# Two cross attentions on one core: products of the identity in the last steps, and the last image outputs added by VectorE

## The chip, the cores and the metric

The kernel runs on one core of a Trainium2 chip. The metric is the time of one execution on the device in microseconds (us). The engines of the core work side by side, each through its own queue of instructions in order: TensorE (products and transpositions), VectorE, ScalarE, GpSimd, and SyncE, which issues most of the transfers.

## What is computed

Two cross attentions in a row, each with 20 heads of 16 channels, over 64 batch entries of 256 tokens and 320 channels, all in float32. The context of an entry has 77 rows of 512 channels. The first attention, cut to what matters:

```python
q, k, v = x @ Wq.T, text @ Wk.T, text @ Wv.T      # by head
out = softmax(q @ k.T / 4) @ v                    # 77 rows of context
x = merge_heads(out) @ Wo.T + bo + x
```

The second treats the last 4 rows of the context as an image:

```python
probs_t = softmax(q @ k_t.T / 4)                  # 73 text rows
text_out = probs_t @ v_t
qsem = l2norm(probs_t @ text)
fused = q @ k_ip.T / 4 + 0.5 * (qsem @ l2norm(ip).T)
ip_out = (softmax(fused) * mask) @ v_ip           # 4 image rows
out = (merge(text_out) + merge(ip_out)) @ W_out + b_out + x
```

The change touches where `merge(ip_out)` is added to `merge(text_out)`, and nothing else that is computed.

## The kernel before, in words

Two batch entries make a pair; there are 32 pairs (NP). A pair takes 10 steps (NU) in each layer: two entries times five units, a unit being eight (entry, head, token block) blocks. The loop at the end of the function runs over steps g from 0 to 344. In step g the first layer works on unit g and the second on unit g - 13 (LAG). So the first layer ends with step 319 and the second layer's scores with step 332; steps 333 to 344 only finish the last pair. The order of instructions on each engine is the order in which the program issues them (keep_order), so a waiting instruction holds back everything behind it on its engine.

One step of the second layer is this. `semantics` (L744, L750) multiplies the transposed weights of the step before with a table of the context and the values; `scores` (L641) multiplies queries and keys. Both write one tile of four PSUM banks, `sc`, of which there is a single buffer. VectorE reads it three times: the maximum (`mx`, L659), the subtraction (`w`, L661), and the product with the weights (`prod`, L761 and L764). ScalarE copies its text sums (`sums`, L1096). Only then may the next step's products write the tile. ScalarE takes the exponential (L672, L673), and TensorE transposes the result in the next step: `transposed` (L705 into `tr`, L706 into `rtr`), copied out by ScalarE (L712, L713). The tiles of all transpositions come from one pool of two buffers, handed out in turn. A transposition is a single instruction `nc.tensor.transpose(to, data, ident)`.

Other work of the pairs is put into the steps by `fillers`, in four lists. Those that matter in the last steps are, with k = g % 10: `queries` (L555 to L570), `text_transposed` (k = 0 and 5; `atr`, L826, copied by L829 and L830), `gram` (k = 6, L493), `image_transposed` (k = 7; `itr`, L903, copied to `iwT` by L905), `image_attend` and `image_attend_last` (k = 8; `ipv`, L915 and L932), `project` (k = 9; `o_ps`, L528, its end L537 in the next step, results added to x by L601), and `project_last` (k = 0 and 2; L616, added by L620). At the end of an entry (step k = 4 or 9 of the second layer's count) its image weights are made: `image_least`, `image_norm` (a square root and an exponential on ScalarE, each with a table load, L863 and L865), `image_scores`, `image_shifted`, `image_exponential` and `image_weights` (L871 to L891 and L839), over ScalarE, VectorE and GpSimd in turn; `text_output` makes `an`, which `text_transposed` reads.

`image_attend` writes two banks (`both`). Its `out_of` has ScalarE copy each to `t` in SBUF (L921), and after the second GpSimd adds all of `t` to the main part of `aT` (L923), which `project` reads.

Of the kernel before, what the change touches and what calls it, by code (L numbers as in the profile page):

```python
# [8 lines left out]
F32 = mybir.dt.float32  # L9
# [13 lines left out]
P = 128  # L23
# [15 lines left out]
NU = 2 * len(UNITS)  # L39
# [24 lines left out]
def tile_two_cross_attentions(ctx: ExitStack, tc: tile.TileContext, a: dict, out: bass.AP):  # L64
# [35 lines left out]
    nc = tc.nc  # L100
    x_in, c_in, cip_in = a["x"], a["ctx"], a["ctx_ip"]
    NB = x_in.shape[1] // S
    NP = NB // 2
# [8 lines left out]
    ptr = ctx.enter_context(tc.tile_pool(name="ptr", bufs=2, space=PSUM))  # L112
# [95 lines left out]
    def load_more(g):  # L208
        queue = nc.sync
        if g == 1:  # L210
            queue.dma_start(cip, cip_in.rearrange("(k p) t -> p k t", p=P))
            load_ctx_weight("wkip1", queue, wkip)
        elif g == 3:
            load_ctx_weight("wvip1", queue, wvip)
        elif g == 5:
            wo[0], bo[0] = load_out("wo0", queue), load_bias("bo0", queue)
        elif g == 6:
            wq[1] = load_chan("wq1", queue)
        elif g == 8:
            wo[1], bo[1] = load_out("wo1", queue), load_bias("bo1", queue)  # L220
            queue.dma_start(smask, a["smask"])


    ident = const.tile([P, P], F32, tag="ident", name="ident")
# [99 lines left out]
    kTs, kbds, qs, vips, aTs = {}, {}, {}, {}, {}  # L324
# [304 lines left out]
    def eight(t, u):  # L629

        return t[:, PLACES[u] : PLACES[u] + 8].rearrange("p (r e) ... -> p r e ...", e=2)
# [65 lines left out]
    def transposed(l, p, b, u, w):  # L697

        n = P if l else 8 * R0
        part, s = UNITS[u]  # L700
        flat = w.rearrange("p i j t -> p (i j t)") if l else w
        ps = ptr.tile([P, 4, P], F32, tag="tr", name=f"tr{l}_{p}_{b}{u}")
        pr = ptr.tile([P, 4, P], F32, tag="tr", name=f"rtr{l}_{p}_{b}{u}")
        for i in range(4):
            nc.tensor.transpose(ps[:, i, :], flat[:, i * P : (i + 1) * P], ident)  # L705
        nc.tensor.transpose(pr[:n, 0, :], flat[:, 4 * P : 4 * P + n], ident)  # L706
        if l:
            pts[1] = (
                sp.tile([P, 4, P], F32, tag="pt1", name=f"pt1_{p}_{b}_{u}"),
                sp.tile([n, P], F32, tag="pr1", name=f"pr1_{p}_{b}_{u}"),  # L710
            )
            nc.scalar.copy(pts[1][0], ps)  # L712
            nc.scalar.copy(pts[1][1], pr[:n, 0, :])  # L713
            return
        if part == 2:
            pt, rt = pts[0, 2, b] = (
                sp.tile([P, 2, S], F32, tag="pt2", name=f"pt2_{p}_{b}"),
                sp.tile([n, P], F32, tag="pr2", name=f"pr2_{p}_{b}"),
            )
            nc.scalar.copy(  # L720
                pt.rearrange("p l (s t) -> p s l t", s=2), ps.rearrange("p (s l) t -> p s l t", s=2)
            )
            nc.scalar.copy(rt, pr[:n, 0, :])
            return
        if s == 0:
            pts[0, part] = (
                sp.tile([P, 4, S], F32, tag="pt0", name=f"pt0_{p}_{b}_{part}"),
                sp.tile([n, S], F32, tag="pr0", name=f"pr0_{p}_{b}_{part}"),
            )
        pt, rt = pts[0, part]  # L730
        nc.scalar.copy(pt[:, :, s * P : (s + 1) * P], ps)  # L731
        nc.scalar.copy(rt[:, s * P : (s + 1) * P], pr[:n, 0, :])

    def semantics(ps, start, stop, p, b, u, rows):

        part, _ = UNITS[u]
        pt, rt = rows
        for i in range(4):  # L740
            for j in range(2):
                half_rows = slice(j * M, (j + 1) * M)
                at = SEM0 + i // 2 * GV
                nc.tensor.matmul(  # L744
                    ps[:, i % 2 * 2 + j, at : at + GV], pt[half_rows, i, :], gv[b][half_rows, part, i, :],
                    start=start and i < 2, stop=False,
                )
        for r in range(4):
            quarter = slice(r * QR, (r + 1) * QR)
            nc.tensor.matmul(  # L750
                ps[:, r, SEM0 : SEM0 + 2 * GV].rearrange("p (e d) -> p e d", d=GV)[:, :, M:],
                rt[quarter, :], gr[b][quarter, part], start=False, stop=stop,
            )
# [154 lines left out]
    def image_attend(p):  # L908

        wT = made["wT"]  # L910
        both = [pms.tile([P, 512], F32, tag="ms", name=f"ipv{p}_{i}") for i in range(2)]
        for b in range(2):
            for i in range(2):
                rows = slice(i * QR, (i + 1) * QR)
                nc.tensor.matmul(  # L915
                    both[i][:, b * S : (b + 1) * S], vips[p, b][rows, i * P : (i + 1) * P],
                    wT[rows, b * S : (b + 1) * S], start=True, stop=True,
                )

        def out_of(i):  # L920
            nc.scalar.copy(t[:, i, :], both[i])  # L921
            if i:
                nc.gpsimd.tensor_add(aTs[1, p][0], t, aTs[1, p][0])  # L923

        t = big.tile([P, 2, S2], F32, tag="ip_out", name=f"ip_out{p}", bufs=1)
        return [lambda i=i: out_of(i) for i in range(2)]
# [110 lines left out]
    def unit(g):  # L1037
        return (g // NU, g % NU // len(UNITS), g % len(UNITS)) if 0 <= g < NP * NU else None
# [11 lines left out]
    for g in range(NP * NU + LAG + 12):  # L1050
        p, k = divmod(g, NU)
        first, second, third, begin = fillers(k, p)
        if g == NU + 3:
            in_order = len(nc.cur_bb.bb.instructions)
        load_more(g)
        now = [unit(g), unit(g - LAG)]
        ps = prod = None
        for fn, args in early.pop(g, ()):
            fn(*args)
        drains = [fn for what in ("q", "o") if what in held for fn in held.pop(what)()]  # L1060
        if now[0] or now[1] or before1:
            ps = psc.tile([P, 4, 512], F32, tag="sc", name=f"sc{g}")
            todo = []
            if before1:
                todo.append((semantics, (*before1[:3], before1[4])))
            for l in range(2):
                if now[l]:
                    todo.append((scores, (l, *now[l])))
            for n, (fn, args) in enumerate(todo):
                fn(ps, n == 0, n == len(todo) - 1, *args)  # L1070
        for fn, args in begin:
            fn(*args)
        if "i" in held:
            drains += held.pop("i")()
        for fn in drains:
            fn()
        for l in range(2):
            if now[l]:
                shifted(ps, l, *now[l])
        new1 = None  # L1080
        if last1:
            transposed(1, *last1)
            new1 = (*last1, pts[1])
        if now[0] and k != 5:
            exponential(0, g, *now[0])
        if before1:
            prod = weighted(ps, *before1[:4])
        for fn, args in first:
            fn(*args)
        if last0:  # L1090
            transposed(0, *last0)
        if now[0] and k == 5:
            exponential(0, g, *now[0])
        ends = before1 and before1[2] == len(UNITS) - 1
        if before1:
            nc.scalar.copy(eight(stats[before1[:2]][1], before1[2]), by_block(ps)[:, :, :, TT:])  # L1096
            if ends:
                image_least(*before1[:2])
        if now[1]:
            exponential(1, g, *now[1])  # L1100
        for fn, args in later.pop(g, ()):
            fn(*args)
        if now[0]:
            normalize(g)
        if before1:
            q, b, u = before1[:3]
            nc.vector.tensor_reduce(eight(stats[q, b][2], u), prod, AX.X, ALU.add)  # L1107
            if ends:
                image_squares(q, b)
                made["an"] = text_output(q, b)  # L1110
                later[g + 1] = [(image_scores, (q, b))]
                early[g + 2] = [(image_shifted, (q, b)), (image_exponential, (q, b))]
                early[g + 3] = [(image_weights, (q, b))]
        for fn, args in second:
            fn(*args)
        if last0:
            q, b, u, _ = last0
            if u == 1 or u == len(UNITS) - 1:
                attend(q, b, int(u > 1))
        for fn, args in third:  # L1120
            fn(*args)
        if ends:
            image_norm(*before1[:2])
        last0 = (*now[0], ws[0]) if now[0] else None
        before1 = new1
        last1 = (*now[1], ws[1]) if now[1] else None
# [51 lines left out]
```

## Time and profile before

| | us |
|---|---|
| median of 3 runs (2629.02 to 2631.37) | 2630.31 |
| the profiled execution's own time | 2628.61 |
| its span, first to last instruction | 2626.9 |
| TensorE busy | 2549.2 (97%) |
| VectorE busy | 1969.9 (75%) |
| ScalarE busy | 1538.8 (59%) |
| GpSimd busy | 1442.4 (55%) |
| TensorE's share of the chain that ended last | 87% |
| mean granted clock of TensorE | 0.986 |

A matmul's end is modelled, so neighbouring matmuls overlap in the records; how fast they follow each other is read from their starts. A product in float32 leaves two records, a transposition one. The page cuts the span into 40 equal slices of 66 us; a digit is the busy share in tenths, and the row PEclk is the share of TensorE's full clock that was granted. In a timeline a row has its start, its length, engine, line and tiles, and in brackets the idle time before it and what ended it. In a table of stretches each row is one stretch, with busy time and count for each engine, then the granted clock, the share of the transfer engines and GB/s.

### The profile page before, as it was taken

The numbers are of one execution on the slowest core, as the hardware profiler recorded it, in microseconds if no ns is written. First come the engines' busy times: TensorE is split into PE (matmuls) and PEld (weight loads), VectorE is DVE, ScalarE is ACT, GpSimd is POOL, SyncE is SP. The second block draws the span as 40 slices with busy tenths as digits, with TensorE's granted clock in tenths as the row PEclk, the third lists the DMA queues.
The fourth block names the chain that finished last, engine by engine and source line by source line (L and its number), as shares of the span: only waits on it lengthen the run. The fifth ranks groups of instructions, "written<-read, shape, count | busy, mean of one in ns | idle before, by whom it ended". The sixth has DMA issues, their size and how long they took to land.

```text
span 2626.9 us, 73603 instructions
## 1 busy us (share of the span) xinstructions
PE 2549.2 (97%) x26792; PEld 1974.0 (75%) x26792; DVE 1969.9 (75%) x3639; ACT 1538.8 (59%) x3991; POOL 1442.4 (55%) x3515
## 2 busy tenths in 40 slices
PE   7999999999999999999999999999999999999897
PEld 5677777777777777777777777777777777777675
DVE  3577777777777777777777777777777777777864
ACT  3465665655665665665665665655665655665643
POOL 2455555565555565555565555565555565555542
PEclk9999999999999999999999999999999999999986
DMA  5212211112111112111112111112111112111000
GB/s 163 72 29 58 58 42 47 42 51 57 57 44 47 42 51 58 58 42 48 42 52 57 58 42 48 41 52 58 58 42 48 41 52 58 56 38 36 26 22 23
DMA packets 154657, 132.24 MB, mean 50 GB/s; under 512 B 48249, under 2 KB 132985, under 8 KB 154297
## 3 DMA queue, kind: packets, MB, share of 16 engines
q1 hardware_dynamic: 153432, 126.38, 16.8%
q8 instruction: 215, 3.52, 0.5%
q10 hardware_dynamic: 864, 1.15, 0.1%
q14 instruction: 146, 1.19, 0.1%
HBM read 89.53 MB, written 33.91 MB: 47 GB/s over the span
## 4 chain that ended last, share of the span: by engine, by line
PE 87%; DVE 6%; ACT 3%; DMA 1%; issue 1%; POOL 1%; SPq 0%; POOLq 0%; DVEq 0%; ACTq 0%
PE sc L744 13%; PE tr L705 11%; PE o_ps L528 8%; PE sc L641 7%; PE v_ps L379 6%; PE sc L750 5%; PE q_ps L555 4%; PE q_ps L528 4%; PE k_ps L334 4%; PE o_ps L616 3%; PE o_ps L537 3%; PE pv L777 2%; DVE w L661 2%; PE q_ps L557 2%; PE q_ps L563 2%; PE rtr L706 2%
## 5 line engine op out<-in xcount | busy, mean ns | idle before, releaser
L659 DVE TENSOR_REDUCE mx<-sc 128x8 f32<-128x584 f32 (+1 forms) x640 | 497.6, 778 | 460.1 <-PE sc L641 460.0
L692 POOL TENSOR_TENSOR parts<-w,sm 128x512 f32<-128x512 f32 (+1 forms) x640 | 439.6, 708 | 301.6 <-ACT parts L673 180.7
L661 DVE TENSOR_TENSOR w<-sc,mx 128x616 f32<-128x616 f32 x640 | 511.9, 800 | 66.7 <-DVE mx L659 0.5
L712 ACT COPY pt<-tr 128x512 f32<-128x512 f32 x320 | 186.8, 584 | 449.3 <-PE tr L705 437.5
L705 PE MATMUL tr<-ident,parts 128*128 128x128 f32 x2560 | 412.8, 284 | 12.8 <-POOL parts L692 5.2
L744 PEld LDWEIGHTS sc<-gv,pt 64*128 64x128 f32 x5120 | 323.5, 191 | 117.2 <-ACT sums L1096 67.5
L744 PE MATMUL sc<-gv,pt 64*128 64x94 f32 x5120 | 363.3, 282 | 35.1 <-ACT sums L1096 32.7
L705 PEld LDWEIGHTS tr<-ident,parts 128*128 128x128 f32 x2560 | 284.5, 142 | 124.6 <-issue 88.8
L676 POOL COPY att<-w 128x32 f32<-128x32 f32 x320 | 66.8, 209 | 469.7 <-DVE w L661 469.0
L669 ACT ACTIVATE w<-w 128x616 f32<-128x616 f32 x320 | 232.0, 725 | 96.3 <-DVE w L661 95.4
L687 DVE TENSOR_REDUCE sm<-w 128x8 f32<-128x616 f32 x320 | 248.2, 776 | 13.5 <-ACT w L669 13.5
L641 PE MATMUL sc<-kbd,q 32*128 32x154 f32 x5120 | 250.0, 308 | 1.0 <-ACT q L586 0.8
L528 PE MATMUL o_ps<-aT,wo 128*128 128x256 f32 x1024 | 234.3, 383 | 1.6 <-POOL aT L923 1.6
L1107 DVE TENSOR_REDUCE nrm<-prod 128x8 f32<-128x584 f32 x320 | 227.4, 711 | 0.4
L761 DVE TENSOR_TENSOR prod<-sc,parts 128x512 f32<-128x512 f32 x320 | 218.0, 681 | 5.5 <-PE sc L750 5.5
L528 PEld LDWEIGHTS o_ps<-aT,wo 128*128 128x128 f32 x1024 | 192.0, 193 | 25.8 <-POOL aT L923 2.4
L672 ACT ACTIVATE parts<-w 128x512 f32<-128x512 f32 x320 | 206.8, 646 | 0.0
L641 PEld LDWEIGHTS sc<-kbd,q 32*128 32x128 f32 x5120 | 188.5, 188 | 6.0 <-issue 5.0
L731 ACT COPY pt<-tr 128x512 f32<-128x512 f32 x256 | 150.6, 588 | 67.5 <-PE tr L705 66.8
L379 PE MATMUL v_ps<-wv,cf 128*128 128x320 f32 (+1 forms) x624 | 182.1, 438 | 0.0
L706 PE MATMUL rtr<-ident,parts 128*104 128x128 f32 (+1 forms) x640 | 175.9, 275 | 0.0
L1096 ACT COPY sums<-sc 128x168 f32<-128x168 f32 x320 | 96.6, 302 | 118.9 <-DVE prod L764 118.0
(148 smaller groups left out, 4802.9 us busy)
## 6 DMA issues: line engine op xcount, KB each, us to landing
vip<-vip_rows SPq DMA_DIRECT2D x1280, 5.0 KB
out_dram<-x SPq DMA_DIRECT2D x64, 256.0 KB
x<-in_x_dram SPq DMA_DIRECT2D x31, 512.0 KB
v_rows<-vs SPq DMA_DIRECT2D x38, 320.0 KB
vm<-v_rows SPq DMA_DIRECT2D x152, 80.0 KB
ct<-in_ctx_dram SPq DMA_DIRECT2D x32, 308.0 KB
cf<-in_ctx_dram SPq DMA_DIRECT2D x38, 256.0 KB
g_rest<-gram_rest SPq DMA_DIRECT2D x512, 0.5 KB
```

The costliest lines, as they stand in the source:

```text
L379: nc.tensor.matmul(ps[:n, :C], cfs[i][:, k, :n], wv[l][:, k, :], start=(k == 0), stop=(k == KE - 1))
L528: nc.tensor.matmul(ps[b][:, m, :], w[:, k, m * P : (m + 1) * P], main[:, k, b * S : (b + 1) * S], start=(k == 0 and m == 0), stop=False,)
L641: nc.tensor.matmul(ps[:, r, 2 * T * l : 2 * T * (l + 1)], q[rows, b, :] if part == 2 else q[rows, t0 : t0 + P], kbd[rows, part].rearrange( ...
L659: nc.vector.tensor_reduce(mx, sc[:, :, :, :nt], AX.X, ALU.max)
L661: nc.vector.tensor_tensor(w, sc, mx.unsqueeze(3).broadcast_to([P, 4, 2, T]), ALU.subtract)
L669: nc.scalar.activation(w, w, AF.Exp, scale=SCALE)
L687: nc.vector.tensor_reduce(sm, w, AX.X, ALU.add)
L692: nc.gpsimd.tensor_tensor(two[:, 8 * t0 : 8 * t1].rearrange("p (h t) -> p h t", h=8), w[:, :, t0:t1], sm.unsqueeze(2).broadcast_to([P, 8, ...
L705: nc.tensor.transpose(ps[:, i, :], flat[:, i * P : (i + 1) * P], ident)
L706: nc.tensor.transpose(pr[:n, 0, :], flat[:, 4 * P : 4 * P + n], ident)
L744: nc.tensor.matmul(ps[:, i % 2 * 2 + j, at : at + GV], pt[half_rows, i, :], gv[b][half_rows, part, i, :], start=start and i < 2, stop=False,)
L1107: nc.vector.tensor_reduce(eight(stats[q, b][2], u), prod, AX.X, ALU.add)
```

## The change

A helper `keep_busy(n)` takes a tile from the pool of transpositions and writes n transpositions of the identity into it; nobody reads them. It is called in every step after 322, after the step's transpositions and first fillers: with 14 while the second layer has scores (323 to 332), then with 12, 16, 14, 16 and 16 (333 to 337). For the last pair, `out_of` no longer copies and adds over ScalarE and GpSimd; VectorE adds each bank of `both` to its half of `aT`.

```diff
+    def keep_busy(n):
+        if n:
+            ps = ptr.tile([P, 4, P], F32, tag="tr", name=f"busy{len(busy)}")
+            busy.append(n)
+            for i in range(n):
+                nc.tensor.transpose(ps[:, i % 4, :], ident, ident)
+
+    busy = []
...
         def out_of(i):
+            main = aTs[1, p][0]
+            if p == NP - 1:
+                nc.vector.tensor_add(main[:, i, :], both[i], main[:, i, :])
+                return
             nc.scalar.copy(t[:, i, :], both[i])
             if i:
-                nc.gpsimd.tensor_add(aTs[1, p][0], t, aTs[1, p][0])
+                nc.gpsimd.tensor_add(main, t, main)
...
         if last0:
             transposed(0, *last0)
+        idle = g - NP * NU
+        if idle > 2:
+            keep_busy(14 if now[1] else {13: 12, 14: 16, 15: 14, 16: 16, 17: 16}.get(idle, 0))
```

## The prediction

> **What bounds the kernel now.** I read the 40 slices first. TensorE is busy everywhere, at full clock except in the last slices:
>
> ```profile
> PE   7999999999999999999999999999999999999897
> PEclk9999999999999999999999999999999999999986
> ```
>
> So the change bears on the last 90 us or so. I cut them into steps, from one step's first product L744 to the next one's. The columns are us, busy us (count) of TensorE, of its weight loads, VectorE, ScalarE and GpSimd, then the granted clock:
>
> ```profile
> 2527.50:2534.18 6.68, 6.68 (x62) 4.46 (x61) 3.06 (x5) 2.67 (x7) 1.79 (x6) 1.00 0.06 21
> 2534.18:2538.95 4.77, 2.53 (x39) 2.06 (x38) 2.70 (x5) 1.74 (x5) 0.02 (x1) 1.00 0.00 0
> 2545.41:2551.55 6.14, 5.57 (x46) 4.87 (x45) 3.15 (x7) 2.87 (x11) 1.33 (x4) 0.50 0.01 3
> 2574.03:2578.65 4.62, 4.62 (x58) 3.31 (x54) 4.29 (x10) 1.87 (x6) 1.41 (x3) 1.00 0.30 114
> 2578.65:2583.34 4.69, 2.53 (x38) 2.03 (x38) 3.91 (x9) 2.80 (x11) 1.69 (x4) 1.00 0.13 31
> 2583.34:2589.45 6.11, 4.49 (x37) 3.60 (x37) 3.69 (x8) 1.74 (x6) 1.22 (x5) 0.51 0.00 1
> ```
>
> These are steps 323, 324, 326, 330, 331 and 332. A light step takes 4.7 us at full clock and 6.1 at half. Each is a ring: products into the one score bank, VectorE's maximum, subtraction and product (L659, L661, L761), ScalarE's sums (L1096), next products. The clock halves TensorE's part only: 1.76 us of products at 1.00, 3.2 at 0.50.
>
> Next, what sets the clock. It changes at 2539.06, 2569.78, 2583.43 and 2617.57, which are 9, 4 and 10 times 3.41 us apart, so I cut time on that grid. First all work, in the same columns:
>
> ```profile
> 139.49:142.90 3.41, 2.64 (x40) 1.92 (x36) 2.33 (x4) 1.09 (x3) 3.41 (x6) 1.00 0.25 69
> 142.90:146.32 3.42, 1.03 (x16) 1.00 (x16) 3.25 (x7) 2.48 (x7) 0.89 (x4) 1.00 0.57 173
> 146.32:149.73 3.41, 3.41 (x35) 3.07 (x34) 2.32 (x5) 3.00 (x5) 3.29 (x7) 0.50 0.05 15
> 2559.54:2562.96 3.42, 3.42 (x28) 2.47 (x27) 1.77 (x3) 0.24 (x1) 0.64 (x3) 0.50 0.01 0
> 2562.96:2566.37 3.41, 3.41 (x23) 2.32 (x21) 1.72 (x4) 2.47 (x7) 2.44 (x2) 0.50 0.04 10
> 2566.37:2569.78 3.41, 3.41 (x29) 2.84 (x28) 1.37 (x2) 0.44 (x1) 1.24 (x3) 0.50 0.06 15
> 2569.78:2573.20 3.42, 3.42 (x18) 2.76 (x18) 2.21 (x6) 2.74 (x7) 1.34 (x4) 1.00 0.05 12
> ```
>
> The main transpositions (L705) alone in three of these (us, TensorE, weight loads, ScalarE, clock):
>
> ```profile
> 139.49:142.90 3.41, 1.28 (x8) 0.84 (x8) 0.58 (x1) 1.00 0.25 69
> 2559.54:2562.96 3.42, 0.34 (x2) 0.34 (x3) 0.00 (x0) 0.50 0.01 0
> 2566.37:2569.78 3.41, 1.11 (x4) 0.72 (x4) 0.44 (x1) 0.50 0.06 15
> ```
>
> A stretch with little work is followed by one at half clock: 1.03 us busy (above), 1.13 (60.98), 1.17 (2535.65) and 1.26 (2580.02) all lost it; 1.47 (54.16) kept it. Coming back takes much more than staying: 3.42 us busy at 2559.54 did not suffice.
>
> [...] Stretch 139.49 has about 1.1 us of other work (2.64 less about 1.5 of L705 and L706), no more than stretches that lost the clock, and kept it. And the clock came back after 2566.37, with about 2.1 us of other work and 1.3 of transpositions, not after 2559.54 with 3.1 of other work and 0.34. (Amount is not all: 2562.96, with 0.77 of L705, stayed cold.) I let them count. [...]
>
> **The change part by part.** 214 transpositions: 14 in each of steps 323 to 332, then 12, 16, 14, 16, 16 in 333 to 337. Length of one: after 0.16 us for the first, L705 and L826 follow each other every 0.11 us at full clock (two of L826 in 0.38 us, of which the last is 0.27) and 0.22 at half. A weight load takes 0.14, overlapped in those rows. I take 0.11: 14 cost 1.6 us, 12 cost 1.4, 16 cost 1.8; at 0.14 they cost 2.0, 1.7 and 2.3.
>
> The new tile takes the buffer of the step's own transposition, so the products wait for ScalarE's copy L712. Behind them in TensorE's queue stand the step's later products (L555, atr, gram, itr, L932) and the next step's scores. From the scores' end: transposition 0.66, hand-over 0.09, copy 0.58, hand-over 0.15, so 1.48 until they start. A light step becomes 1.76 + 1.48 + 1.6 = 4.85 us, just above its ring of 4.7. Step by step, against the times between the L744 of before (all at full clock):
> - 323: TensorE is busy throughout, so 1.6 is paid: 6.68 to 8.26. 324: 4.77 to 4.85.
> - 325: the copy stands behind two table loads on ScalarE (L863 to L865, 3.04 us), starts 3.6 us in, is done at 4.2; 1.6 of products and 0.82 of atr follow: 6.46 to 6.75.
> - 326: 4.85 + 0.6 of gram: 6.14 to 5.45. 327: 4.85 + 0.5 of itr: 6.17 to 5.35.
> - 328: ipv takes 1.0 at full clock; two copies L921 (1.07) precede L712, so the products start at 4.65, and L932 adds 0.55: 7.21 to 6.8.
> - 329: 1.76 + 0.65 + 3.55 (o_ps) + 1.6 + 0.96: 9.10 to 8.5.
> - 330: already at full clock and full: 4.62 to 6.2. 331: 4.69 to 4.85.
> - 332: 6.11 to 4.85. 333: 1.44 + 1.48 + 1.4: 4.80 to 4.3. Scores of 334: 2.66 to 1.44.
>
> Sum: 323 to 325 lose 1.95, 326 to 329 gain 2.5, 330 and 331 lose 1.75, 332 to 334 gain 3.0. Net gain 1.8 us: the products eat most of what the clock gives here.
>
> The end, after step 334's scores (2596.91):
>
> ```profile
> 2607.30 2.52 PE L915 MATMUL ipv<-iwT,vip 32*128 32x256 f32 x8 [0.67 <-ACT iwT L905]
> 2609.42 1.07 ACT L921 COPY ip_out<-ipv 128x512 f32<-128x512 f32 x2 [2.17 <-PE ipv L915]
> ...
> 2610.57 2.34 POOL L923 TENSOR_TENSOR aT<-ip_out,aT 128x1024 f32<-128x1024 f32 x1 [4.43 <-ACT ip_out L921]
> ...
> 2612.96 5.98 PE L528 MATMUL o_ps<-aT,wo 128*128 128x256 f32 x16 [1.61 <-POOL aT L923]
> ```
>
> - Until itr, ScalarE, VectorE and GpSimd work 8.85 us in a row; the clock doesn't matter. Beside it TensorE does 30 products (3.3), atr (0.8, whose data are there at 3.3), waits for copies of atr (until 5.0), 32 more (3.6): done at 8.7. Hidden, with nothing to spare; without that cover each 0.1 us would count. itr's first half, now behind them, still ends before the last iw comes. Gain 0.1.
> - ipv start to o_ps start is 5.66. After: ipv at full clock has its first bank after 1.0, then two VectorE additions of 128x512. No row shows this one. Nearest are L936, the same addition at half the size, 417 ns, and L761, the same size with one operand from PSUM, 681 ns. Bounds: L921's 0.54 per copy, and twice L936, 0.83. I take 0.68 each: 1.0 + 1.36 + 0.1 = 2.45. L932 (0.55), now waiting for the first addition, ends before the second. Gain 3.2 (2.9 to 3.5).
> - o_ps 5.91 at mostly half clock becomes 3.55, as at 2516.41. Gain 2.35. What follows (8.03) is at full clock already.
>
> Gain 1.8 + 0.1 + 3.2 + 2.35 = 7.5 us. On the profiled execution: span 2626.9 to 2619.4, time 2628.61 to 2621.1. The median is 1.7 above that execution, so 2630.3 - 7.5 = 2622.8 us.
>
> **Rivals.**
> - *The transpositions don't count, the clock falls, and they run at half speed on TensorE's path* (slower). Then 14 cost 3.2 us. Steps 325 to 328 lose about 3.3 each, 329 2.4, 332 and 333 2.2 each, 323 and 330 1.6 each; at the end 62 of them (13.8 us) plus atr (1.5) exceed the 8.85 they should hide in: itr 7 later, less 2 from VectorE's additions. Sum 13.2 + 2.4 + 4.4 + 3.2 + 5 = about +28: 2658 us. It decides once transpositions count so little that a stretch is worth under about 1.3 us busy: a light step's other work is 1.76 of 4.85 us, 1.24 per stretch of 3.41. [...] Against: the two pairs of stretches. 12%.
> - *Held, but each costs a whole weight load, 0.14*. Steps 323 to 333 pay 0.4 more each (4.2), the end about 1: gain 2.2, 2628.1 us. A brief dip lands here too: step 325 now has 1.9 us of idle TensorE before its products, leaving 1.5 us busy in a badly placed stretch, next to the 1.47 that held and the 1.26 that didn't; one stretch at half clock costs 1.7 us or less. For it: 0.14 per load in every row. Against: products 0.11 apart in L705, L826. 20%.
> - *More than forecast*: starts on the copies earlier than I put them, or VectorE's additions at 0.54: 2619 us or below. 8%.
> - *As forecast*: 60%, with its own range 2619.5 to 2626.
>
> **The numbers.** About 5.3 us, 0.2%, is what a measurement of this kernel can tell from no change: the border is 2625.05. The forecast's 60% gives 0.54 faster and 0.06 same; the second rival 0.03 faster, 0.16 same, 0.01 slower; the third 0.08 faster; the first 0.12 slower. Faster 0.65, same 0.22, slower 0.13. The range, 2618.5 to 2630, holds forecast and second rival; outside are the first rival and the best cases.
>
> **What would show it.** Right: clock 1.00 in every slice to the end; L744 to L744 near 4.85 us in the light steps, 8.3 in 323 and 6.2 in 330; itr waiting for GpSimd's iw and not for TensorE; 2.4 us from ipv to o_ps; o_ps 3.6 long. Wrong: 0.50 in the middle of the stretch, transpositions 0.22 or 0.14 apart, itr behind them by over 0.5 us, or additions over 0.83 us each.

## The result and the profile after

The changed kernel takes 2626.45 us (median of 14 runs, 2623.81 to 2630.66), the kernel before beside it 2630.73 (14 runs): 4.3 us less. The ratio is 0.9988, which is 3.2 us, with an interval of 0.9979 to 0.9996, which is 5.5 to 1.1 us: faster, but by little. Forecast were 7.5 us. The time lies in the forecast's range, but it misses the likeliest case, whose own range ends at 2626, by 0.45, and it stays above the border of 2625.05 under which the forecast would have called it faster. The gain falls between that of the likeliest case and the second rival's 2.2.

The profiled execution took 2627.7 us, its span is 2626.0. TensorE's row and the clock's in the 40 slices of the changed kernel's page:

```profile
PE   7999999999999999999999999999999999999998
PEclk9999999999999999999999999999999999999999
```

In the clock, the last two slices have gone from 8 and 6 to 9. The same six steps as before (323, 324, 326, 330, 331 and 332), in the same columns:

```profile
2532.41:2540.58 8.17, 8.17 (x77) 5.95 (x76) 3.07 (x5) 2.68 (x7) 1.80 (x6) 1.00 0.06 18
2540.58:2545.41 4.83, 4.21 (x53) 3.55 (x52) 2.77 (x5) 1.80 (x5) 0.09 (x1) 1.00 0.00 0
2551.87:2557.18 5.31, 4.75 (x61) 4.17 (x60) 3.27 (x6) 3.09 (x10) 0.47 (x2) 1.00 0.01 3
2577.71:2583.85 6.14, 6.14 (x71) 4.79 (x68) 5.22 (x12) 1.93 (x7) 1.85 (x4) 1.00 0.26 95
2583.85:2588.62 4.77, 4.20 (x52) 3.54 (x52) 3.05 (x6) 2.30 (x9) 0.68 (x2) 1.00 0.08 18
2588.62:2593.45 4.83, 4.21 (x53) 3.55 (x52) 3.73 (x8) 1.77 (x6) 1.22 (x5) 1.00 0.00 2
```

Step 326 fell from 6.14 to 5.31 and step 332 from 6.11 to 4.83, because their clock is 1.00; step 323 rose from 6.68 to 8.17 and step 330 from 4.62 to 6.14, because TensorE was full there already. The first column shows something else: step 323 starts at 2532.41, 4.9 us later than in the trace of before, and nothing is changed up to there. The whole gain after that point, 99.4 to 93.6 us, is nearly lost between the two profiled spans (2626.9 and 2626.0). The runs below find where the 4.9 come from.

The clock of this trace changes at 145.27, 152.09, 2473.16, 2483.40, 2613.10 and 2616.52, which are 2, 680, 3, 38 and 1 times 3.4133 us apart; in between it is 0.50 or 1.00. The stretches of 3.41 us, now on the grid of this execution:

```profile
2599.45:2602.87 3.42, 3.42 (x33) 3.28 (x31) 2.02 (x5) 2.54 (x4) 1.38 (x4) 1.00 0.00 0
2609.69:2613.10 3.41, 3.07 (x14) 1.83 (x15) 1.66 (x3) 0.00 (x0) 0.00 (x0) 1.00 0.00 0
2613.10:2616.52 3.42, 3.42 (x10) 2.72 (x9) 0.06 (x1) 0.00 (x0) 0.00 (x0) 0.50 0.00 0
```

The new transpositions alone in the first two of these (us, TensorE, weight loads, clock):

```profile
2599.45:2602.87 3.42, 3.22 (x30) 2.98 (x28) 1.00 0.00 0
...
2609.69:2613.10 3.41, 0.00 (x0) 0.00 (x0) 1.00 0.00 0
```

In the first stretch TensorE did nothing but transpose (the 3 records that are not new are the atr of `text_transposed`), 3.42 us long, and it kept the clock. The second was busy for 3.07 of 3.41 us and lost it. The end of the timeline, to be set beside the one of before:

```profile
2609.53 1.97 PE L926 MATMUL ipv<-iwT,vip 32*128 32x256 f32 x8 [0.67 <-ACT iwT L916]
...
2611.09 1.29 DVE L934 TENSOR_TENSOR aT<-ipv,aT 128x512 f32<-128x512 f32 x2 [3.76 <-PE ipv L926]
...
2611.84 0.86 PE L947 MATMUL ipv<-iwT,vip 80*64 80x256 f32 x4 [0.34 <-DVE aT L934]
...
2612.63 5.41 PE L528 MATMUL o_ps<-aT,wo 128*128 128x256 f32 x16
```

o_ps now follows ipv after 3.10 us in place of 5.66, but it still takes 5.34 in place of 5.91, since the stretch after 2613.10 is at half clock. (L926 and L947 are L915 and L932 of before; L934 is the new addition.)

### The profile page after: what moved, and what is told of

Same layout as the page of the kernel before. It is cut to its first block, busy times and chain, and to the rows that moved or that the text cites. A ratio compares the mean times of both kernels' runs of the same rounds, so it can differ in the third digit from the quotient of the medians.

```text
span 2626.0 us, 74027 instructions
## 1 busy us (share of the span) xinstructions
PE 2558.2 (97%) x27006; PEld 1981.0 (75%) x27006; DVE 1972.3 (75%) x3641; ACT 1539.2 (59%) x3989; POOL 1440.1 (55%) x3514
## 4 chain that ended last, share of the span: by engine, by line
PE 85%; DVE 7%; ACT 3%; DMA 2%; issue 1%; POOL 1%; SPq 1%; DVEq 0%; POOLq 0%; ACTq 0%
PE sc L755 12%; PE tr L705 11%; PE o_ps L528 8%; PE sc L641 7%; PE v_ps L379 6%; PE sc L761 4%; PE q_ps L528 4%; PE q_ps L555 4%; PE k_ps L334 4%; PE o_ps L616 3%; PE o_ps L537 3%; PE pv L788 2%; DVE w L661 2%; PE q_ps L563 2%; PE q_ps L557 2%; DVE mx L659 2%
## 5 line engine op out<-in xcount | busy, mean ns | idle before, releaser
L705 PE MATMUL tr<-ident,parts 128*128 128x128 f32 x2560 | 410.4, 283 | 11.1 <-POOL parts L692 5.3
L755 PEld LDWEIGHTS sc<-gv,pt 64*128 64x128 f32 x5120 | 317.9, 188 | 108.8 <-ACT sums L1114 60.3
L755 PE MATMUL sc<-gv,pt 64*128 64x94 f32 x5120 | 357.6, 279 | 27.9 <-ACT sums L1114 27.7
L705 PEld LDWEIGHTS tr<-ident,parts 128*128 128x128 f32 x2560 | 283.0, 141 | 122.2 <-issue 87.0
L676 POOL COPY att<-w 128x32 f32<-128x32 f32 x320 | 66.8, 209 | 471.9 <-DVE w L661 471.4
L528 PE MATMUL o_ps<-aT,wo 128*128 128x256 f32 x1024 | 233.4, 381 | 0.0
L528 PEld LDWEIGHTS o_ps<-aT,wo 128*128 128x128 f32 x1024 | 190.7, 191 | 24.0 <-DVE aT L934 0.4
L1114 ACT COPY sums<-sc 128x168 f32<-128x168 f32 x320 | 96.6, 302 | 120.2 <-DVE prod L775 119.0
```

The lines of the kernel that those rows point to most:

```text
L528: nc.tensor.matmul(ps[b][:, m, :], w[:, k, m * P : (m + 1) * P], main[:, k, b * S : (b + 1) * S], start=(k == 0 and m == 0), stop=False,)
L755: nc.tensor.matmul(ps[:, i % 2 * 2 + j, at : at + GV], pt[half_rows, i, :], gv[b][half_rows, part, i, :], start=start and i < 2, stop=False,)
```

## The experiments

*The theory.* The transpositions hold the clock; each costs TensorE 0.11 us where TensorE is the bound; VectorE's additions shorten the way to o_ps; and what counts for the clock is how much of the array works, not how long TensorE is busy. *Rivals:* one half of the change does all; busy time alone counts; what is gained after step 323 is only the scatter of the part before it.

"Region" is the time from the first L744 of step 323 to the end of the span: 99.4 us before, 93.6 in the changed kernel. "Early" is when step 323 starts. Ratios are against the kernel before, measured beside each, with 95% intervals. Columns are in us; region, o_ps (its length) and early come from one trace each.

| | region | o_ps | early | median, us | ratio |
|---|---|---|---|---|---|
| VectorE's additions only | 97.0 | 4.87 | 2532.1 | 2630.55 | 1.0002 (0.9990 to 1.0013) |
| the same again | 96.9 | 5.39 | 2529.7 | 2628.43 | 0.9985 (0.9973 to 0.9996) |
| transpositions only | 96.6 | 6.34 | 2531.6 | 2630.07 | 1.0001 (0.9993 to 1.0010) |
| more around ipv | 91.9 | 3.65 | 2534.0 | 2625.90 | 0.9991 (0.9980 to 1.0002) |
| none in full steps | 87.5 | 3.65 | 2530.9 | 2623.57 | 0.9976 (0.9968 to 0.9984) |
| fewer, more around ipv, and 10 in step 314 | 87.5 | 3.65 | 2531.2 | 2619.20 | 0.9958 (0.9942 to 0.9973) |
| 7 in place of 14 | 89.7 | 6.06 | 2529.5 | 2622.29 | 0.9972 (0.9961 to 0.9982) |
| 32 rows in place of 128 | 126.6 | 6.07 | 2530.1 | 2658.35 | 1.0102 (1.0068 to 1.0135) |
| full products of 128 rows | 94.2 | 5.05 | 2533.2 | 2627.68 | 0.9990 (0.9982 to 0.9999) |
| fewer, more around ipv, step 314, and 7 for 14 | 91.1 | 3.65 | 2528.4 | 2618.14 | 0.9949 (0.9937 to 0.9962) |
| before, once more (one run) | 99.4 | 6.01 | 2529.2 | 2630.33 | |
| before with blank lines | 96.5 | 6.03 | 2531.9 | 2630.64 | 1.0001 (0.9993 to 1.0010) |

**Each half alone.** First the additions without the transpositions.

```diff
-        if idle > 2:
+        if False:
             keep_busy(...)
```

> VectorE's additions kept, no products of the identity at all. The measure is the region from the first semantics product of step 323 to the end of the span: 99.4 us before, 93.6 in the changed kernel. Theory (the products hold the clock, the additions shorten the way from ipv to o_ps): the clock is 0.50 for most of the region as before, steps 323 to 333 take 66.7 as before, ipv start to o_ps start falls from 5.66 to about 3.6 (ipv at half clock 2.0, two additions 0.68 each, the second one's end), o_ps stays near 5.9. Region 97.3, time about 2 us below before. Rival (the additions bring all of it and the products nothing): region 93.6, time 4 to 6 below before.

The region is 97.0, as the theory had it (97.3), with the steps as before (66.8 us for 323 to 333). ipv to o_ps took 4.25 and not 3.6: at half clock the last part of ipv (L947 here, L932 before), which now waits for the first addition, holds TensorE for 1.4 us and is itself the last to end. o_ps starts behind it, at 2616.21:

```profile
2614.81 1.47 PE L947 MATMUL ipv<-iwT,vip 80*64 80x256 f32 x4 [0.36 <-DVE aT L934]
```

The rival falls. Of the 2.4 us gained, 1.4 come from this way; 1.0 is a shorter o_ps, which the edit doesn't explain (0.5 in the second trace). The gain was not seen in the time, though; so the kernel was run a second time, see below.

Then the transpositions with the last pair's outputs as before.

```diff
-            if p == NP - 1:
-                nc.vector.tensor_add(main[:, i, :], both[i], main[:, i, :])
-                return
```

> Products of the identity kept, the image outputs of the last pair again over ScalarE and GpSimd. Theory: clock 1.00 from 323 until after ipv, steps 323 to 333 take 65.3 as in the changed kernel, ipv to o_ps about 5.1 (1.6 for ipv, 1.07 for the two copies, 2.35 for GpSimd), and as TensorE idles some 2.5 us there the clock falls to 0.50 for o_ps (5.3 to 5.9). Region 95.5 to 96, time 3 to 4 below before. Rival (scatter of the earlier part only): region 99 or more.

The clock was 1.00 from 2482.8 to 2612.5. Steps 323 to 333 take 65.3, as in the changed kernel, and o_ps follows ipv after 5.14, where it was 5.66: the way over ScalarE and GpSimd is hardly shortened by the clock. Behind a wait of 2.08 us o_ps ran at half clock for 5.5 of its 6.34. Region 96.6: the steps and the scores of 334 bring 2.6, the rest 0.2. So in one trace each the halves gain 2.4 and 2.8 us, and together 5.8. These sizes are rough, since a region of 96.5 also came up without any edit (blank lines, below). As with the first, the time doesn't show the region's gain.

**The lost clock at the end.**

```diff
+        if p == NP - 1:
+            keep_busy(6)
         wT = big.tile([n, S2], F32, tag="iwT", name=f"iwT{p}", bufs=1)
...
-            keep_busy(... 17: 16} ...)
+            keep_busy(... 17: 16, 18: 4} ...)
```

> The changed kernel with 10 more transpositions of the identity: 6 behind itr, where TensorE waits 0.67 us for the copy, and 4 between ipv and its last part, where it waits 0.34. Theory (the clock fell at 2613.1 because products of 32 rows count little, so the stretch with ipv was too light): with 10 transpositions more the clock holds through o_ps, which takes 3.6 in place of 5.33: region 91.8, time 1.8 below the changed kernel. Rival (the weak stretch is ipv itself, and 4 to 10 transpositions don't lift it): o_ps still 5.3, region 93.6 to 93.9.

o_ps took 3.65 and the region is 91.9. From the timeline of this kernel:

```profile
2611.10 2.00 PE L928 MATMUL ipv<-iwT,vip 32*128 32x256 f32 x8
2613.03 0.66 PE L741 MATMUL busy<-ident 128*128 128x128 f32 x4
2613.62 0.65 PE L949 MATMUL ipv<-iwT,vip 80*64 80x256 f32 x4
2614.20 3.72 PE L528 MATMUL o_ps<-aT,wo 128*128 128x256 f32 x16
```

The waits of 0.67 and 0.34 are filled. That alone isn't proof: in the next run o_ps also took 3.65 without these ten, where the grid fell so that the stretch with ipv held the start of o_ps too. In all three kernels that have them the clock held; of the four that lack them but keep the rest of the change (changed, fewer, half, full products) it was lost in three. Likely, then, not shown. In the time it can't be told: 2625.90 beside 2626.45.

**Fewer.**

```diff
-        if idle > 2:
+        if idle > 2 and idle not in (3, 9, 10):
```

> The changed kernel without the 14 products in steps 323, 329 and 330, which are full of other work. Theory: each paid 1.6 us there on TensorE's path and the clock doesn't need them: steps 6.68, 6.9 and 4.6, region 93.6 - 4.8 = 88.8, clock 1.00 in between, time 4.8 below the changed kernel. Rival (the clock needs them: without those of 323 it falls at 324 or 325): 0.50 somewhere in 324 to 328, region 93 or more.

The theory held to the tenth in the steps. Steps 323, 324, 325, 329 and 330 of this kernel:

```profile
2530.91:2537.60 6.69, 6.69 (x63) 4.46 (x62) 3.06 (x5) 2.67 (x7) 1.81 (x6) 1.00 0.07 23
2537.60:2542.42 4.82, 4.20 (x52) 3.54 (x51) 2.76 (x5) 1.79 (x5) 0.08 (x1) 1.00 0.00 0
2542.42:2548.89 6.47, 4.88 (x58) 4.19 (x58) 4.38 (x10) 5.41 (x12) 3.38 (x9) 1.00 0.01 1
2566.23:2573.12 6.89, 6.89 (x64) 5.85 (x64) 4.00 (x8) 3.24 (x7) 2.34 (x7) 1.00 0.07 13
2573.12:2577.73 4.61, 4.61 (x57) 3.30 (x53) 4.28 (x10) 2.61 (x7) 2.22 (x5) 1.00 0.32 120
```

The clock is 1.00 throughout and the three full steps are back at 6.7, 6.9 and 4.6: 4.5 us less, and 1.7 more because o_ps had the full clock. These full steps needed no filling.

**Earlier too.** In the trace of the changed kernel step 315 ran at half clock after TensorE had waited 2.26 us in step 314. These are steps 314 and 315 of the changed kernel, and the same two of before:

```profile
2466.71:2473.30 6.59, 4.33 (x59) 3.83 (x58) 4.52 (x8) 3.23 (x9) 3.92 (x7) 0.99 0.11 29
2473.30:2483.47 10.17, 9.61 (x73) 6.82 (x73) 7.93 (x16) 7.43 (x17) 5.44 (x11) 0.50 0.00 1
```

```profile
2465.25:2471.78 6.53, 4.27 (x60) 3.77 (x59) 4.46 (x8) 3.23 (x9) 3.85 (x7) 1.00 0.10 29
2471.78:2478.57 6.79, 5.26 (x73) 3.87 (x73) 6.43 (x13) 6.09 (x13) 3.85 (x9) 1.00 0.00 1
```

The same work in step 314, and 3.4 of the 4.9 us are lost in step 315. The next kernel adds 10 transpositions in step 314 and takes the two edits above.

```diff
+        if idle == -6:
+            keep_busy(10)
-        if idle > 2:
+        if idle > 2 and idle not in (3, 9, 10):
```

> Three edits to the changed kernel at once: no products in the full steps 323, 329 and 330; 10 more around ipv; and 10 in step 314, where TensorE waits 2.26 us in every trace and after which the clock fell in five of six of them (step 315 took 8.6 to 10.2 us there, 6.8 where the clock held). Theory (a stretch that is too light is followed by half clock, wherever it lies): step 315 at 6.8, first product of 323 at 2527.5 to 2530 in place of 2531 to 2534, region 87.5, time about 2619, 11 us below before. Rival (the scatter of the earlier part has another cause than step 314): 323 starts at 2531 or later, time 2623 as without the third edit.

Step 315 took 6.8 and the median is 2619.2, the ratio 0.9958 (0.9942 to 0.9973). But step 323 started at 2531.2, as the rival had it: the clock fell at 2493.1 instead, in steps 317 and 318, and it had been low for 10.2 us in the first 152. So step 314 is one of several places, and filling one of them doesn't end the scatter. The ten runs say more for it than the one trace. By their mean clock they spent 13 us at half clock on average, against 19 to 25 in the six versions that hold the clock in the last steps without the ten in step 314. Their median is 4.4 us below that of "none in full steps", whose region is as long, though the ten around ipv differ as well.

**How much.**

```diff
-            keep_busy(14 if now[1] else ...)
+            keep_busy(7 if now[1] else ...)
```

> The changed kernel with 7 products in place of 14 in each of steps 323 to 332. Theory (7 are enough to stay, as staying takes less than coming back, and each costs 0.11 us where TensorE is the bound): clock 1.00 through 323 to 337, steps 323 and 325 to 330 each 0.8 shorter, 324, 331 and 332 near their ring of 4.7: region 93.6 - 5.6 = 88.0. Rival (14 are needed): 0.50 somewhere in 325 to 333, region 92 or more.

With 7 the clock held through 323 to 333 and these took 60.1 us, 5.2 less than with 14. It was lost behind itr, in a stretch with ipv again, so o_ps took 6.06 and the region is 89.7 in place of the 88.0 expected.

**Rows or busy time.** Two kernels replace each pair of transpositions by one product of the identity with itself, which leaves two records and keeps TensorE busy about as long (14 records in 1.66 us at 128 rows, 14 transpositions in 1.58). One uses 32 rows, the other all 128.

```diff
-                nc.tensor.transpose(ps[:, i % 4, :], ident, ident)
+                if i % 2 == 0:
+                    nc.tensor.matmul(ps[:, i % 4, :], ident[:QR, :], ident[:QR, :], start=True, stop=True)
```

> The changed kernel with each pair of transpositions replaced by one product of 32 rows of the identity (two records), so TensorE is busy equally long but with a quarter of its rows. Theory (rows count, busy time doesn't): the clock falls in 324 or 325 and stays at 0.50 for long, region 105 or more. Rival (only busy time counts): clock 1.00, steps as in the changed kernel, region 93 to 94.

Region 126.6, and 2658.35 us: a ratio of 1.0102 (1.0068 to 1.0135). This is what the first rival of the forecast said of instructions that don't count, price and all (2658): steps 323 to 333 take 22.1 us more than before (23.2 in the rival's sum), the rest 5.1 (5). Three stretches of it, of all work, in the columns used before:

```profile
2545.17:2548.58 3.41, 1.89 (x18) 1.63 (x15) 3.12 (x6) 3.17 (x9) 1.41 (x4) 1.00 0.00 0
2548.58:2551.99 3.41, 3.41 (x19) 2.85 (x19) 0.43 (x2) 1.42 (x6) 1.05 (x3) 0.50 0.02 5
2551.99:2555.41 3.42, 3.42 (x35) 2.93 (x31) 0.77 (x1) 0.39 (x2) 0.00 (x0) 0.50 0.00 0
```

A stretch with 1.89 us busy lost the clock, and two full stretches didn't bring it back. It stayed low for 37.5 and then 44.4 us. In the kernel before, 1.47 us of products of 128 rows had kept it:

```profile
54.16:57.57 3.41, 1.47 (x6) 0.72 (x4) 3.08 (x6) 0.88 (x2) 1.37 (x2) 1.00 0.46 128
```

> The control for the products of 32 rows: the same 7 products (14 records) per step, with all 128 rows of the identity. Theory (rows count, and a product and a transposition of 128 rows count alike): clock 1.00 through 323 to 337, steps as in the changed kernel within 0.1 each, region 92 to 94, depending on whether the stretch with ipv is hit. Rival (what the run with 32 rows lost came from using products at all, or from the waits): 0.50 from step 325 on, region above 105.

The edit is the same without the two `[:QR, :]`. Region 94.2, clock 1.00 from step 323 to ipv, ratio 0.9990 (0.9982 to 0.9999). Its step 325, which took 7.84 us with 32 rows, at a mean clock of 0.83:

```profile
2546.33:2552.80 6.47, 4.96 (x59) 4.27 (x58) 4.29 (x10) 5.33 (x12) 3.28 (x9) 1.00 0.00 1
```

Most steps are 0.1 longer than in the changed kernel, as the 14 records take 1.66 us where 14 transpositions take 1.58. So it isn't product against transposition, nor the waits: the two kernels of this comparison differ in the rows alone.

**All edits, with 7.**

> The version with fewer, earlier and later products, with 7 in place of 14 in steps 324 to 328, 331 and 332. Theory: the clock holds with 7, steps 325 to 328 are 0.6 to 0.75 shorter, 324, 331 and 332 0.1 to 0.3: region 87.5 - 3.2 = 84.3, time about 2616. Rival (half is too little in some phases of the grid): 0.50 in 325 to 333, region 87.5 or more.

The rival held in the profiled execution: the clock fell at 2544.2 and for 10.2 us at 2561.3, and the region is 91.1. The stretch before the first fall, and the one after it:

```profile
2540.79:2544.20 3.41, 1.80 (x27) 1.31 (x26) 2.32 (x6) 3.29 (x6) 1.79 (x4) 1.00 0.00 0
2544.20:2547.61 3.41, 3.41 (x21) 3.08 (x21) 1.26 (x4) 2.27 (x8) 1.49 (x3) 0.51 0.02 5
```

It ends in step 325, where the copy stands behind the table loads. The same 7 held there in the run with 7 alone, on another place of the grid. The median is 2618.14, ratio 0.9949 (0.9937 to 0.9962), from 5 runs; against 2619.2 with 14 that is no difference these runs can tell. Both lie 7 to 8 us below the changed kernel in the median, and 0.0030 and 0.0039 in the ratio.

**The part before step 323.** Three kernels that bring no new edit: the one before once more, the same with blank lines put in, and VectorE's additions only, as in the first experiment.

> The kernel before once more, unchanged, for a second trace of it. Theory (the 4.9 us by which the changed kernel was late at step 323 is not the change but step 315 at half clock, which the first trace of before happened to escape): step 315 at 8.6 to 10.2 in this trace, first product of 323 at 2530 or later, region 99.4 again. Rival (the change itself delays the earlier part): 323 at 2527.5 as in the first trace.

> The kernel before with blank lines put in and no other edit: what a comparison shows when nothing has changed. Question: in ten traces of edited kernels step 323 starts at 2528.4 to 2534.0 (mean 2531.3), in two of the kernel before at 2527.5 and 2529.2, though the instructions up to there are the same. Theory A (chance: where half-clock stretches fall in the first 2530 us differs from execution to execution): ratio 1.000 within 0.001, 323 starts anywhere from 2527.5 to 2534, later the more half clock there was before. Theory B (the kernel before is special and any other program is later there by 2 to 3 us): ratio 1.001, 323 at 2531 or later.

> VectorE's additions alone a second time, since the first run showed 2.4 us gained after step 323 and none in the time. Theory A (chance in the earlier part): ratio 0.999, median about 2 us below before, region 97.0 again. Theory B (the earlier part is later in an edited program): ratio 1.000, 323 at 2531 or later again.

The first expectation was wrong in its detail: step 315 took 6.8 again, and step 323 started at 2529.2. With blank lines step 315 took 8.8 and step 323 started at 2531.9, as late as in the edited kernels, and the ratio is 1.0001. Nor was the region fixed: the clock happened to come back for a while at 2554, and the region was 96.5. And the additions gave 0.9985 (0.9973 to 0.9996) the second time, where the first gave 1.0002; by the mean clock of their runs the same kernel spent 68 and 75 us at half clock. This speaks for Theory A: the earlier part differs by chance. A small part of Theory B isn't excluded: the nine edited kernels without the ten in step 314 start step 323 at 2531.5 on average, the three traces of the kernel before at 2529.5. In all 14 traces its length goes with the time at half clock before step 323, by the clock's records:

| half clock before 323, us | step 323 starts at, us |
|---|---|
| 6.8 (2 traces) | 2527.5, 2528.4 |
| 10.2 (3) | 2529.2, 2529.7, 2530.1 |
| 13.7 (2) | 2529.5, 2531.2 |
| 17.1 (5) | 2530.9, 2531.6, 2531.9, 2532.1, 2532.4 |
| 20.5 (2) | 2533.2, 2534.0 |

The first trace of before stands in the first row and that of the changed kernel in the fourth. That is where the 4.9 us come from, 3.4 of them in step 315. The times of whole executions go the same way: over the 128 runs of the kernel before that were measured beside these experiments, the time and the half-clock time (from each run's mean clock) have a correlation of 0.96.

## Why the prediction was right in its mechanism, and where it wasn't in size

| term | forecast gain | in the two traces |
|---|---|---|
| steps 323 to 333 | 0.6 | 1.4 |
| scores of step 334 | 1.2 | 1.1 |
| from there to ipv | 0.1 | 0.1 |
| ipv to o_ps | 3.2 | 2.6 |
| o_ps | 2.35 | 0.6 |
| after that | 0 | 0.0 |
| sum | 7.5 | 5.8 |

- *The transpositions count for the clock.* Right, and reading this from the trace of before, by two pairs of stretches, decided the sign. A stretch of nothing but transpositions kept the clock (3.42 us busy, 2599.45 to 2602.87), and products of 128 rows in their place made no difference to it (1.00 from step 323 to ipv). No run shows the term that the first rival's sum starts from, transpositions that don't count: the kernel with them took 2626.45 us and not 2658. What took that long was the run with products of 32 rows, 2658.35.
- *What each costs.* 0.11 forecast, 0.113 measured (14 in 1.58 us, 2536.32 to 2537.90). Every step came within 0.3 us of its forecast: 8.17 for 8.26, 4.83 for 4.85, 6.46 for 6.75, 5.31 for 5.45, 6.14 for 6.2. The copy behind the table loads in 325 was there, with a wait of 1.59 us.
- *The 62 that hide behind ScalarE, VectorE and GpSimd.* They did, with nothing to spare, as said.
- *ipv to o_ps.* The step "ipv at full clock has its first bank after 1.0" failed: it came after 1.57. The records follow each other in pairs 0.44 us apart, one product each, and they had done so at half clock too (0.43 to 0.44 before), so the clock had less to give here. The additions themselves took 0.69 and 0.68, for 0.68 forecast. That L932 "ends before the second" failed as well: it took 0.79 in place of 0.55, and o_ps started behind it at 2612.63, where the second addition had ended at 2612.38.
- *"o_ps 5.91 at mostly half clock becomes 3.55."* This is the term that was mis-sized: 5.34. I had counted a stretch safe when TensorE was busy for over 1.3 to 1.5 us of it; the one with ipv had 3.07 and lost the clock, which cost o_ps 1.8 us. Busy time was the wrong measure: 1.8 of those 3.07 are products of 32 rows. "Coming back takes much more than staying" rests on the same measure and fails with it (last section). When the stretch holds (more around ipv, none in full steps), o_ps takes 3.65.
- *From the profile to the median.* In the trace of before that the 5.8 us are counted from, the clock ran low for all of step 325 to 328; with blank lines alone one execution of the same instructions had 2.9 us less there. Three traces of the kernel before have regions of 99.4, 99.4 and 96.5, mean 98.5, so an average gain near 4.9; measured 4.3 by the medians and 3.2 by the ratio.
- *What was luck.* The errors of the terms cancel in part: the steps gave 0.8 more than forecast, the way from ipv to o_ps 0.6 less and o_ps 1.75 less. Of the forecast's own signs of being right, the lengths of the steps and itr's wait for GpSimd's iw came. The clock of 1.00 to the end, 2.4 us from ipv to o_ps and 3.6 for o_ps did not. That the time is inside the range, 2618.5 to 2630, owes much to its width. (One sum of the first rival is off: 62 at 0.22 us are 13.6, not 13.8; nothing hangs on it.)

## What to carry to other kernels

In this kernel's last steps TensorE waited in a regular rhythm and the granted clock was mostly at half. There unread products in its waits were worth more than they cost, but only in the light steps: where TensorE was the bound already they were paid in full (4.5 us, beside a gain of 5.8). Elsewhere, look in the trace for the same two signs, and judge a stretch by how many rows of the array worked in it, not only by how long TensorE was busy: here the same 7 products a step kept the clock at 1.00 in step 325 with 128 rows, and with 32 rows its mean there was 0.83. And a gain of a few us in the last 100 of 2630 is read from that region in the trace; the time of one execution carries several us of chance from places that the change doesn't touch (step 323 started anywhere from 2527.5 to 2534.0 in the 14 traces).

## What the runs showed of the hardware that was not expected

- The products of 32 rows didn't hold the clock where as many of 128 rows did. Beside the run with 32 rows (1.89 us busy, lost) stand 3.07 us with ipv (lost), and 1.47 us of products of 128 rows (kept, in the kernel before). An estimate over all 14 traces says what separates such stretches. Count each record of TensorE as 0.11 us per 128 moving columns (at full clock L705 follows at 0.11 and L528, with 256 columns, at 0.22), times its share of 128 rows and of 128 columns of the loaded operand, in the stretch that it starts in. Of the 10,719 stretches of 3.41 us, the 132 with under 1.09 us of such work were all followed by half clock, and the 10,479 with over 1.4 all by full clock; the 108 between went either way, 54 to 54. (In the traces of before and of the changed kernel alone: 17, 1,495 and 18 of 1,530.) These are borders of the count in this kernel. The run with 32 rows had 0.80 in its stretch; the other two, with 3.07 and 1.47 us busy, had 1.10 each, at the edge.
- In this count, coming back takes no more than staying. The 55 stretches at half clock that were followed by full clock had 1.18 us or more of such work, and the 127 that weren't had 1.32 or less. At half clock a product is busy for longer (0.475 us for a record of L705, 0.273 at full clock), so a full stretch can hold too little: the one at 2559.54 had 3.42 us busy and 1.03 us of work, the one at 2566.37, after which the clock came back, 1.44. The count was made after the fact; sizes between 32 and 128 rows, and the share of columns, were not tried alone.
- In ipv of the last pair the products don't follow the clock. The second pair of records and the third start 0.43 to 0.44 us apart in all 14 traces, at half clock as at full. In 29 of the 32 pairs of the kernel before, the eight records start within 0.65 to 0.71 us; in the last pair that takes 1.9 us, and 1.6 in the changed kernel. There four separate semaphore instructions stand before each product in TensorE's queue, 0.106 us apart. That these are the reason is read from the trace and wasn't tried.
- The place of the 3.41 us grid differs from execution to execution (its first border lies 2.96 us into the span in the trace of before, 1.91 in that of the changed kernel), and with it whether a weak stretch is met. Step 315 took 6.8 us in three traces of the same instructions and 8.6 to 10.2 in nine others. In the three, the grid cut TensorE's wait in step 314 in two, and both stretches kept 1.7 us or more of the work counted above; in the nine, one stretch held the wait and had 1.3 or less.
